# A two-layer sequence model on one Trainium2 core: in later blocks of the state-space scan, time steps and decays laid out by (head, token tile), with rows spread by transfers

## The chip, the cores and the metric

The kernel runs on one core of one Trainium2 chip, as one launch. The metric is device time in microseconds (us). The kernel before took 1160.8 us (median of three runs, 1160.18 to 1161.01). One further execution was profiled: 1159.44 us, of which the profile covers a span of 1157.7 us from the first to the last instruction. Engines are named as in the profile: PE (matmul), PEld (its weight loads), DVE (VectorE), ACT (ScalarE), POOL (GpSimd), SP (SyncE, which here only issues transfers).

## The reference, cut to what matters

The model has two layers, each a sequence mixer and a feed-forward part with residual additions and layer norms between them. The change touches only the mixer of layer 0, a state-space scan with 16 heads of width 64 and a state of 16:

```
zxbcdt = hidden @ W_in                  # gate (1024), xBC (1056), dt (16 heads)
xBC  = silu(causal_conv4(xBC))          # x: 16 heads x 64; B: 16; C: 16
dt   = softplus(dt + dt_bias)
dA   = exp(dt * -exp(A_log))            # one decay per token and head
h    = h * dA[t] + (dt[t] * x[t]) B[t]  # state 64 x 16 per head, over 1024 tokens
y[t] = h . C[t]
y    = (y + D_skip * x) * silu(gate);  y = rmsnorm(y) * norm_w;  out = y @ W_out
```

There are 2 sequences of 1024 tokens, so 2048 tokens. All values are float32.

## The kernel before, in words

The tokens are worked on in four blocks of 512 (b = 0 to 3; blocks 0 and 1 are the first sequence, 2 and 3 the second). A block has four token tiles of 128. The recurrence is computed tile by tile: within a tile the scan becomes a matrix product with a lower-triangular matrix of decay products per head, and a state H (64 x 16 per head) is carried from tile to tile.

For each block these parts exist, written as Python generators so that their steps can be woven into each other:

- `head(b)` turns the input (L211), projects B, C and dt (L332, `pbc`) and copies them to `rows` (L338, called rpad in the trace: 48 partitions, B in 0 to 15, C in 16 to 31, dt in 32 to 47). `mix()` runs the convolution of B and C (L243) and its SiLU into `BC`. Then the time steps are turned to tokens on partitions by four small PE transposes (`pdt`, L355), the bias is added (L359), softplus runs on a [128 x 64] tile in 14 DVE instructions and one of ACT (L187 to L198), and the exponent `a` is formed (L364 to L370). Four more transposes (`pa`, L374) turn `a` back to heads on partitions, ACT takes the exponential (L376, `dA`), four DVE scans form the running products `cum` inside each token tile (L388), `dA` with each tile's first column set to zero is written to DRAM (`decays`, L393), and `cum` is split into a rounded and a rest part in `rc` (L395, L398).
- `project(b)` loads the decays of every head back from DRAM, each spread over 128 partitions (L489, four transfers of 1 MB into `L`). It projects the 1024 channels of x in eight steps `inner(m)` (PE L315 `px`, ACT L413 and L285, the convolution on DVE L243 three times, SiLU L291). Between them stand `crows()` (one PE matmul `pc`, L419, and an ACT copy spread C to 128 partitions as CT), `grams()` (the products of B and C, `pgm` L429, and the transposes of B, `pbt` L430), `spans()` (two PE matmuls `pe`, L444, spread `cum` to 8 heads x 16 states; DVE multiplies by CT to give `cdec`, L448, and copies the tile ends to `over`, L449), and, for four heads at a time, `scans()` (ACT copies L to PSUM, L459; DVE scans it against a stacked identity, L465, giving the decay matrices) and `weigh()` (`bdec` on DVE, L475; four POOL multiplies of L by the gram matrix `gm`, L480).
- `recur(b)` does the four token tiles: `py` takes the state through `cdec` (L585) and the tile's own tokens through L (L593), `pst` gives the new state (L603), DVE updates H (L610, L617) and y (L624), and `by_token` prepares the next tile (PE L562, DVE L564, POOL L568).
- `gates(b)` projects the gate (PE L315 `pg`, ACT L635); `gate(b)` multiplies (DVE L643), squares (ACT L645) and sums (POOL L647); `conclude(b)` applies W_out (PE L658 `po`, L667 `pss`), the norm (L671 to L673), layer norm and the store to `x_mid`.

The order of the work: in block 0 (`opening`) PE, DVE and ACT keep the order in which the program is written. From block 1 on a planner orders every queue at compile time by program order and by its own estimate of when operands are ready, and each engine then runs its queue in that order. The steps are woven by hand: `project(b)` is filled with the steps of `conclude(b - 1)`, and `recur(b)` with two steps of `gates(b)` to one of `head(b + 1)`. So the head of block b + 1 runs in the recurrence of block b. PSUM is one pool of eight banks that all parts share; the tags `tmp` (six buffers) and `rows` (two) are shared as well.

Parameters are loaded at the start by SP, ACT and POOL. POOL then builds the identity matrix (masks.py:197, 199), and PE runs 14 matmuls on it (L165) before it turns the first input.

Of the kernel before, what the change touches and what calls it, by code (L numbers as in the profile page):

```python
# [37 lines left out]
def model_kernel(ctx: ExitStack, tc: tile.TileContext, t: dict, out: bass.AP):  # L38
# [6 lines left out]
    xout = out.rearrange("b (k j p) d -> (b k) p j d", p=P, j=NJ)  # L45
    x_mid = tc.dram_tile([NBLK, P, NJ, D], F32, name="x_mid")
    decays = tc.dram_tile([NBLK, NH, TB], F32, name="decays")

    cp = ctx.enter_context(tc.tile_pool(name="const", bufs=1))
    sp = ctx.enter_context(tc.tile_pool(name="small", bufs=2))  # L50
# [52 lines left out]
    cbr = cp.tile([NBC, 1], F32, tag="cbr", name="cbr")  # L103
    nc.gpsimd.dma_start(cbr, cb_src[DI : DI + NBC].rearrange("(p o) -> p o", o=1))
    skips = row("L0_attn_D_skip", NH, dma=nc.gpsimd)
    nc.sync.dma_start(X[1], xin[1])
    w_out = op.tile([P, NX, D], F32, tag="w_out", name="w_out")
    nc.sync.dma_start(w_out, t["L0_attn_W_out"].rearrange("(m p) o -> p m o", p=P))
# [57 lines left out]

    def exponents():
        endless = cp.tile([P, NH], F32, tag="endless", name="endless")  # L170
        nc.vector.tensor_scalar(endless, alog, EXP_MAX, LOG_FLOOR, ALU.is_gt, ALU.mult)
        rootA = cp.tile([P, NH], F32, tag="rootA", name="rootA")
        nc.vector.tensor_scalar(rootA, alog, EXP_MAX, None, ALU.is_le)
        nc.vector.tensor_tensor(rootA, rootA, alog, ALU.mult)
        nc.scalar.activation(rootA, rootA, AF.Exp, scale=0.5)
        rootN = cp.tile([P, NH], F32, tag="rootN", name="rootN")
        nc.vector.tensor_scalar(rootN, rootA, -1.0, None, ALU.mult)
        return endless, rootA, rootN


    def softplus(o, z, n):

        def tmp(k):
            return sp.tile([P, n], F32, tag=f"sp{k}", name=f"sp{k}", bufs=1)

        e, r, s, s2, p = (tmp(k) for k in range(5))
        nc.vector.scalar_tensor_tensor(e, z, -1.0, z, ALU.mult, ALU.min)  # L187
        nc.scalar.activation(e, e, AF.Exp)
        nc.vector.tensor_scalar(r, e, 2.0, None, ALU.add)
        nc.vector.reciprocal(r, r)  # L190
        nc.vector.tensor_tensor(s, e, r, ALU.mult)
        nc.vector.tensor_tensor(s2, s, s, ALU.mult)
        nc.vector.tensor_scalar(p, s2, 1.0 / 15.0, None, ALU.mult)
        for d in (13, 11, 9, 7, 5, 3):
            nc.vector.scalar_tensor_tensor(p, p, 1.0 / d, s2, ALU.add, ALU.mult)
        nc.vector.scalar_tensor_tensor(p, p, 1.0, s, ALU.add, ALU.mult)
        nc.vector.tensor_scalar(r, z, 0.0, None, ALU.max)
        nc.vector.scalar_tensor_tensor(o, p, 2.0, r, ALU.mult, ALU.add)  # L198
# [122 lines left out]
    def head(b, st):  # L321

        if b >= 3:
            X.append(tokens())
            nc.sync.dma_start(X[b], xin[b])
        xT = st["xT"] = transposed(mp, b, X, bufs=2, by_act=b > 0)[0]

        pm = bank("pbc")
        half = TB // 2
        for k in range(NK):  # L330
            for i in range(2):
                nc.tensor.matmul(  # L332
                    pm[i * 64 : i * 64 + NR, :half], w_in[:, k, 2 * DI : IN_DIM],
                    xT[:, k, i * half : (i + 1) * half], start=(k == 0), stop=(k == NK - 1),
                )
        rows = mp.tile([P, 3 + TB], F32, tag="xpad", name="rpad", bufs=3)
        for i in range(2):
            nc.scalar.copy(  # L338
                rows[:NR, 3 + i * half : 3 + (i + 1) * half], pm[i * 64 : i * 64 + NR, :half]
            )  # L340
        BC = st["BC"] = mp.tile([NBC, TB], F32, tag="BC", name="BC")

        mix = started(rows[:, 3:], NBC, b, NX, cwr, cbr, BC, rows)
        if b < 2:
            yield
        if b:
            mix()
            yield

        z = sp.tile([P, NJ, NH], F32, tag="z", name="z")  # L350
        dt = st["dt"] = sp.tile([P, NJ, NH], F32, tag="dt", name="dt")
        a = sp.tile([P, NJ, NH], F32, tag="a", name="a")
        pdt = bank("pdt")
        for j in range(NJ):
            nc.tensor.transpose(  # L355
                pdt[:, j * NH : (j + 1) * NH], rows[32:NR, 3 + j * P : 3 + (j + 1) * P],
                ident[32:NR, 32:NR],
            )
        nc.vector.tensor_tensor(  # L359
            z, pdt[:, : NJ * NH].rearrange("p (j h) -> p j h", h=NH),  # L360
            dtb.unsqueeze(1).to_broadcast([P, NJ, NH]), ALU.add,
        )
        softplus(dt.rearrange("p j h -> p (j h)"), z.rearrange("p j h -> p (j h)"), NJ * NH)
        nc.vector.tensor_tensor(a, dt, rootA.unsqueeze(1).to_broadcast([P, NJ, NH]), ALU.mult)  # L364
        nc.vector.scalar_tensor_tensor(
            a, a, 1.0e18, rootN.unsqueeze(1).to_broadcast([P, NJ, NH]), ALU.min, ALU.mult
        )
        nc.vector.tensor_tensor(a, a, endless.unsqueeze(1).to_broadcast([P, NJ, NH]), ALU.min)
        for lo in (0, 32):
            nc.vector.tensor_scalar(a2[:, :, lo : lo + NH], a, LOG_FLOOR, None, ALU.max)  # L370
        yield
        pa = bank("pa")
        for j in range(NJ):
            nc.tensor.transpose(pa[:NR, j * P : (j + 1) * P], a2[:, j, :], ident)  # L374
        dA, cum = tmp("dA")[:NR], tmp("cum")[:NR]
        nc.scalar.activation(dA, pa[:NR, :], AF.Exp)  # L376
        if b == 0:

            r = st["r"] = mp.tile([NR, TB], F32R, tag="rows", name="rows", bufs=2)
            nc.scalar.activation(r, pa[:NR, :], AF.Exp)  # L380
            yield
            nc.vector.tensor_tensor(r[32:NR], dA[32:NR], r[32:NR].bitcast(F32), ALU.subtract)
            nc.vector.memset(r.bitcast(F32).rearrange("r (j t) -> r j t", t=P)[:, :, 0:1], 0.0)
            mix()
            yield
        for j in range(NJ):
            w = slice(j * P, (j + 1) * P)
            nc.vector.tensor_tensor_scan(  # L388
                cum[:, w], dA[:, w], zeros[:NR].to_broadcast([NR, P]), 1.0, ALU.mult, ALU.add
            )  # L390
        if b:
            nc.vector.memset(dA.rearrange("r (j t) -> r j t", t=P)[:, :, 0:1], 0.0)
            nc.sync.dma_start(decays[b], dA[:NH])  # L393
        rc = st["rc"] = mp.tile([NR, TB], F32R, tag="rows", name="rows", bufs=2)
        nc.scalar.copy(rc, cum)  # L395
        if b == 0:
            yield
        nc.vector.tensor_tensor(rc[32:NR], cum[32:NR], rc[32:NR].bitcast(F32), ALU.subtract)  # L398
        yield

    def parts(b, st):
# [21 lines left out]
        def grams():  # L423

            pgm = bank("pgm")
            pbt = bank("pbt")
            for j in range(NJ):
                s = slice(j * P, (j + 1) * P)
                nc.tensor.matmul(pgm[:, s], BC[:NS, s], st["CT"][:NS, s], start=True, stop=True)  # L429
                nc.tensor.transpose(pbt[:, j * NS : (j + 1) * NS], BC[:NS, s], ident[:NS, :NS])  # L430
            st["gm"] = mp.tile([P, TB], F32, tag="gm", name="gm")
            nc.scalar.copy(st["gm"], pgm)
            st["bt"] = sp.tile([P, NJ, NS], F32, tag="bt", name="bt", bufs=1)
            nc.vector.tensor_copy(
                st["bt"], pbt[:, : NJ * NS].rearrange("p (j n) -> p j n", n=NS)
            )

        def spans():

            cdec = st["cdec"] = mp.tile([P, 2, TB], F32, tag="cdec", name="cdec")  # L440
            over = st["over"] = sp.tile([P, 2, NJ], F32, tag="over", name="over")
            for q in range(2):
                pe = bank("pe")
                nc.tensor.matmul(  # L444
                    pe, pickn[:, 8 * q : 8 * q + 8, :].rearrange("r h n -> r (h n)"), st["rc"],
                    start=True, stop=True,
                )
                nc.vector.tensor_tensor(cdec[:, q, :], pe, st["CT"], ALU.mult)  # L448
                nc.vector.tensor_copy(  # L449
                    over[:, q, :].unsqueeze(2),  # L450
                    pe.rearrange("p (j t) -> p j t", t=P)[:, :, P - 1 : P],
                )

        def scans(h0):

# [28 lines left out]
    def project(b, st):  # L484
# [6 lines left out]
                decays[b, h0 : h0 + 4].rearrange("h t -> (h t)").partition_broadcast(P),  # L491
            )
        inner(0)()
        crows()
        yield
        inner(1)()
        yield
        grams()
        inner(2)()
        yield  # L500
        spans()
        for m in range(3, NX):
            inner(m)()
            if m < 7:
                scans(4 * m - 12)
                weigh(4 * m - 12)
            yield
# [175 lines left out]
    with tc.manual_schedule(  # L683
        engines={mybir.EngineType.PE, mybir.EngineType.DVE, mybir.EngineType.Activation}
    ):
        next(own)
        endless, rootA, rootN = exponents()
        next(own)
        cwx, cbx, normw, dskip = columns_of_layer()
        opening(st, own, g, ahead)  # L690
# [506 lines left out]
```

## Time and profile before

| | us |
|---|---|
| median of the runs | 1160.8 |
| the profiled execution | 1159.44 |
| its span | 1157.7 |
| block 0's opening, about | 0 to 72 |
| recurrence of block 0 | 72 to 103 |
| projection of block 1 | 103 to 167 |
| recurrence of block 1 | 167 to 214 |
| projection, recurrence of block 2 | 214 to 277, 277 to 324 |
| projection, recurrence of block 3 | 324 to 386, 386 to 430 |
| end of the first mixer and all that follows | 430 to 1158 |

The stretches are read from the order of time on PE. In the profile's timeline a line gives the start, the duration, the engine and line of the program, the operation, what it writes and reads, its shape and how many such instructions are merged; in brackets stands idle time of the engine just before and what ended it. A float32 matmul of 512 columns shows as two records, so eight records of L315 are one step of four matmuls. Matmuls are pipelined, so the printed durations of neighbours overlap, and the distance between starts is what one takes of PE's time.

### The profile page before, as it was taken

The page shows a single profiled execution, that of the slowest core. Times are in us where ns is not written, and L with a number is a line of the kernel's source. Part 1 is how long each engine was busy: PE and PEld are TensorE (multiplying, and loading weights), DVE is VectorE, ACT ScalarE, POOL GpSimd, SP SyncE. Part 2 cuts the span into 40 slices and gives each one's busy share as a digit, 9 for nine tenths or more (in the row PEclk, how much of TensorE's full clock was granted, in tenths as well). Part 3 has the DMA queues.
Part 4 walks back from the last instruction along what each step waited for, and adds up shares of the span by engine and source line. Part 5 has one row for each costly group of instructions (what it writes and reads, how often), then busy time and mean ns, then how long its engine had stood idle before and what let it go on. Part 6 is the DMA issues. An engine that isn't in the chain of part 4 may idle for free.

```text
span 1157.7 us, 12317 instructions
## 1 busy us (share of the span) xinstructions
PE 1129.0 (98%) x4659; PEld 686.0 (59%) x4659; DVE 680.7 (59%) x1248; ACT 461.8 (40%) x705; POOL 351.4 (30%) x339
## 2 busy tenths in 40 slices
PE   8999999999999999999999999999999999999995
PEld 5455445445644555654444444447888888888884
DVE  5897795697569756873626328073228765225224
ACT  3334533562354233456645382543223223223222
POOL 1546371445146440367122212237401001001002
PEclk9999999999999999999999999999999999999998
DMA  9003001300030028203000000003501000001001
GB/s 331 2 1 147 1 1 74 147 0 37 1 147 1 37 91 257 99 1 119 0 1 0 1 1 0 1 0 118 182 1 37 1 1 37 1 1 37 1 1 39
DMA packets 30451, 56.46 MB, mean 49 GB/s; under 512 B 11480, under 2 KB 11512, under 8 KB 27824
## 3 DMA queue, kind: packets, MB, share of 16 engines
q1 hardware_dynamic: 29424, 55.45, 13.6%
q8 instruction: 38, 0.62, 0.2%
q14 instruction: 29, 0.24, 0.1%
q10 hardware_dynamic: 864, 0.14, 0.1%
q0 software_dynamic: 96, 0.01, 0.0%
HBM read 47.11 MB, written 8.49 MB: 48 GB/s over the span
## 4 chain that ended last, share of the span: by engine, by line
PE 78%; DVE 15%; ACT 4%; issue 2%; POOL 1%; DVEq 0%; ACTq 0%; POOLq 0%
PE pgu L1041 21%; PE p L890 17%; PE po L1064 10%; PE pg L315 8%; PE px L315 5%; DVE L L465 4%; PE po L967 4%; DVE acc L243 4%; PE po L658 3%; PE py L593 2%; PE po L839 2%; PE pt L211 1%; PE pxt L562 1%; DVE xc L643 1%; DVE st L230 1%
## 5 line engine op out<-in xcount | busy, mean ns | idle before, releaser
L1050 DVE SCALAR_TENSOR_TENSOR h<-pgu,L_ffn_up_scale,sg 128x512 f32<-128x512 f32 x64 | 47.9, 749 | 149.7 <-PE pgu L1041 145.5
L480 POOL TENSOR_TENSOR L<-L,gm 128x512 f32<-128x512 f32 x64 | 93.2, 1485 | 79.6 <-DVE bdec L475 49.6
L315 PE MATMUL px<-xT,w_in 128*128 128x512 f32 x256 | 117.1, 605 | 0.2 <-DVE over L449 0.2
L658 PE MATMUL po<-w_out,xc 128*128 128x512 f32 x256 | 112.6, 593 | 2.0 <-DVE L L465 2.0
L315 PE MATMUL pg<-xT,w_in 128*128 128x512 f32 x256 | 113.5, 594 | 0.0
L890 PE MATMUL p<-xT,w 128*128 128x512 f32 x256 | 112.1, 593 | 1.4 <-ACT xT L220 1.4
L890 PE MATMUL p<-cv,w 128*128 128x512 f32 x256 | 111.0, 592 | 0.0
L1064 PE MATMUL po<-wd,hh 128*128 128x512 f32 x256 | 101.4, 396 | 0.0
L1041 PE MATMUL pgu<-wF__4499,wg 128*128 128x512 f32 x256 | 101.3, 396 | 0.0
L1064 PE MATMUL po<-wd,hl 128*128 128x512 f32 x256 | 101.3, 396 | 0.0
L1041 PE MATMUL pgu<-wF__4499,wu 128*128 128x512 f32 x256 | 101.0, 394 | 0.0
L1041 PE MATMUL pgu<-lo__4500,wg 128*128 128x512 f32 x256 | 100.8, 394 | 0.0
L1041 PE MATMUL pgu<-lo__4500,wu 128*128 128x512 f32 x256 | 100.7, 393 | 0.0
L1048 ACT ACTIVATE sg<-pgu,L_ffn_gate_scale 128x512 f32<-128x512 f32 x64 | 44.0, 687 | 133.3 <-PE pgu L1041 133.2
L1056 ACT CAST hh<-h 128x512 fp32r<-128x512 f32 x64 | 39.8, 621 | 118.5 <-DVE h L1050 118.3
L658 PEld LDWEIGHTS po<-w_out,xc 128*128 128x128 f32 x256 | 48.3, 190 | 63.4 <-issue 55.9
L890 PEld LDWEIGHTS p<-cv,w 128*128 128x128 f32 x256 | 48.4, 190 | 59.8 <-issue 58.8
L315 PEld LDWEIGHTS px<-xT,w_in 128*128 128x128 f32 x256 | 48.0, 193 | 60.5 <-issue 56.8
L890 PEld LDWEIGHTS p<-xT,w 128*128 128x128 f32 x256 | 48.5, 190 | 58.7 <-issue 55.2
L243 DVE SCALAR_TENSOR_TENSOR acc<-xpad,cols,acc 128x512 f32<-128x512 f32 x72 | 68.8, 963 | 18.8 <-ACT acc L285 18.0
L315 PEld LDWEIGHTS pg<-xT,w_in 128*128 128x128 f32 x256 | 47.4, 190 | 54.3 <-issue 53.6
L1138 POOL TENSOR_TENSOR x<-x,r 128x512 f32<-128x512 f32 x12 | 15.2, 1298 | 206.3 <-DVE r L1137 206.3
(239 smaller groups left out, 1944.3 us busy)
## 6 DMA issues: line engine op xcount, KB each, us to landing
L<-decays SPq DMA_DIRECT2D x12, 1024.0 KB, 8.6
x_mid<-x SPq DMA_DIRECT2D x4, 1024.0 KB, 3.8
x<-x_mid SPq DMA_DIRECT2D x4, 1024.0 KB, 4.9
st<-in_L_ffn_gate_w_dram SPq DMA_DIRECT2D x8, 512.0 KB, 4.7
st<-in_L_ffn_up_w_dram SPq DMA_DIRECT2D x8, 512.0 KB, 4.4
st<-in_L_ffn_down_w_dram SPq DMA_DIRECT2D x8, 512.0 KB, 4.0
x<-_attn_hidden_states_dram SPq DMA_DIRECT2D x3, 1024.0 KB, 9.7
out_dram<-x SPq DMA_DIRECT2D x3, 1024.0 KB, 4.3
```

The costliest lines, as they stand in the source:

```text
L243: nc.vector.scalar_tensor_tensor(acc, xpad[:, k : k + TB], w[:, k : k + 1], acc, ALU.mult, ALU.add)
L315: nc.tensor.matmul(pm[:n, :], w_in[:, k, lo : lo + n], xT[:, k, :], start=(k == 0), stop=(k == NK - 1),)
L465: nc.vector.tensor_tensor_scan(L[:, h, :], pl, id4.rearrange("p j t -> p (j t)"), 0.0, ALU.mult, ALU.add)
L480: nc.gpsimd.tensor_tensor(L[:, h, :], L[:, h, :], st["gm"], ALU.mult)
L658: nc.tensor.matmul(po, xc[:, m, j * P : (j + 1) * P], w_out[:, m, :], start=(m == 0), stop=(m == NX - 1),)
L890: nc.tensor.matmul(pm, w1[:, i, k, m * P : (m + 1) * P], rhs[:, k, :], start=(k == 0), stop=(k == NK - 1),)
L967: nc.tensor.matmul(po, y[:, k, j * P : (j + 1) * P], w1[:, 4, k, :], start=(k == 0), stop=(k == NK - 1),)
L1041: nc.tensor.matmul(pm, w[g][:, k, cols], x[:, k, :], start=(k == 0 and x is pieces[0]), stop=(k == NK - 1 and x is pieces[-1]),)
L1048: nc.scalar.activation(sg, pgu[0], AF.Silu, scale=gs[:, m : m + 1])
L1050: nc.vector.scalar_tensor_tensor(h, pgu[1], us[:, m : m + 1], sg, ALU.mult, ALU.mult)
L1056: nc.scalar.copy(hh, h)
L1064: nc.tensor.matmul(po[j], x[:, j * P : (j + 1) * P], wd[m // GK][:, m % GK, :], start=(m == 0 and x is h[0]), stop=(m == NF - 1 and x is h ...
```

## The change

For blocks 1 to 3:

- The dt rows are copied by a transfer inside SBUF from [16 heads, 512 tokens] to `turn`, [64 partitions = (head, token tile), 128 tokens]. Bias, softplus, exponent and exponential run there (`by_rows`), with parameters as columns on those 64 partitions (`by_hj`, loaded at the start by two POOL transfers). One DVE scan gives all running products. They go to DRAM (`since`), and the decays as before.
- The rows of B are copied to the other 64 partitions of `turn`, and one PE transpose (`ptk`) gives both the time steps and B by token (`tk`), in place of the `pdt`, `pa` and `pbt` transposes.
- C goes to DRAM (`crow`) and is read back spread over 128 partitions as CT, in the tag `rows`; the matmul `pc` and its copy go.
- `spans()` reads the running products from `since`, spread to 8 heads x 16 states, straight into `cdec` (two transfers of 256 KB); the `pe` matmuls go, and so do `rc` and its split. The multiply by CT is done on POOL, in place, and `spans()` is called in step m = 6 of the projection, ahead of the last `scans` and `weigh`, and not before step 3.

Block 0 keeps its way; some of its tiles get other buffers.

```diff
+    HJ = NH * NJ
+    by_hj = cp.tile([HJ, 5], F32, tag="by_hj", name="by_hj")
+    for i, name in enumerate(("L0_attn_dt_bias", "L0_attn_A_log")):
+        nc.gpsimd.dma_start(
+            by_hj[:, i : i + 1], t[name].unsqueeze(1).to_broadcast([NH, NJ]).unsqueeze(2)
+        )
...
+        if b:
+            turn = mp.tile([P, P], F32, tag="a2", name="turn")
+            nc.sync.dma_start(
+                turn[:HJ], rows[32:NR, 3:].rearrange("h (j t) -> h j t", t=P)
+            )
         if b < 2:
             yield
         if b:
             mix()
+            nc.sync.dma_start(turn[HJ:], BC[:NS].rearrange("n (j t) -> n j t", t=P))
+            nc.sync.dma_start(crow[b], BC[NS:])
+            st["CT"] = mp.tile([P, TB], F32, tag="rows", name="CT", bufs=2)
+            nc.sync.dma_start(st["CT"], crow[b].unsqueeze(0).to_broadcast([8, NS, TB]))
             yield
+            yield from by_rows(b, turn, tk)
+            return
...
+    def by_rows(b, turn, tk):
+        z, work = turn[:HJ], [tmp(f"work{i}")[:HJ] for i in range(2)]
+        e, r, s, s2, p, a, dA, cum = (
+            w[:, i : i + P] for w in work for i in range(0, TB, P)
+        )
+        if b == 1:
+            exponents(*(by_hj[:, i : i + 1] for i in range(1, 5)))
+        bias, _, end, rA, rN = (by_hj[:, i : i + 1] for i in range(5))
+        nc.vector.tensor_scalar(z, z, bias, None, ALU.add)
+        softplus(z, z, P, (e, r, s, s2, p))
+        nc.vector.tensor_scalar(a, z, rA, 1.0e18, ALU.mult, ALU.min)
+        nc.vector.tensor_scalar(a, a, rN, end, ALU.mult, ALU.min)
+        nc.vector.tensor_scalar(a, a, LOG_FLOOR, None, ALU.max)
+        nc.scalar.activation(dA, a, AF.Exp)
+        nc.vector.tensor_tensor_scan(
+            cum, dA, zeros[:HJ].to_broadcast([HJ, P]), 1.0, ALU.mult, ALU.add
+        )
+        nc.sync.dma_start(since[b].rearrange("h (j t) -> (h j) t", t=P), cum)
+        nc.vector.memset(dA[:, 0:1], 0.0)
+        nc.sync.dma_start(decays[b].rearrange("h (j t) -> (h j) t", t=P), dA)
+        yield
+        pt = bank("ptk")
+        nc.tensor.transpose(pt[:, :P], turn, ident)
+        nc.vector.tensor_copy(tk, pt[:, :P].rearrange("p (v n j) -> p v j n", v=2, j=NJ))
+        yield
...
             for q in range(2):
-                pe = bank("pe")
-                nc.tensor.matmul(
-                    pe, pickn[:, 8 * q : 8 * q + 8, :].rearrange("r h n -> r (h n)"), st["rc"],
-                    start=True, stop=True,
-                )
-                nc.vector.tensor_tensor(cdec[:, q, :], pe, st["CT"], ALU.mult)
...
+                h = slice(8 * q, 8 * q + 8)
+                if b:
+                    nc.sync.dma_start(
+                        cdec[:, q, :], since[b, h].unsqueeze(1).to_broadcast([8, NS, TB])
+                    )
+                    pe = cdec[:, q, :]
...
+                ends = pe.rearrange("p (j t) -> p j t", t=P)[:, :, P - 1 : P]
+                if b:
+                    nc.vector.tensor_copy(over[:, q, :].unsqueeze(2), ends)
+                    nc.gpsimd.tensor_tensor(pe, pe, st["CT"], ALU.mult)
...
         inner(0)()
-        crows()
         yield
...
-        spans()
         for m in range(3, NX):
             inner(m)()
+            if m == 6:
+                spans()
             if m < 7:
                 scans(4 * m - 12)
                 weigh(4 * m - 12)
```

## The prediction

> **What bounds the kernel now.** I read the page's busy table first, then the waits of PE, then the chain that ended last, then PE's, DVE's and POOL's order of time through the later scan blocks, and last the first ten microseconds.
>
> ```profile
> PE 1129.0 (98%) x4659; PEld 686.0 (59%) x4659; DVE 680.7 (59%) x1248; ACT 461.8 (40%) x705; POOL 351.4 (30%) x339
> ```
>
> PE is busy for 1129.0 of 1157.7 us. The list of PE's waits adds up to about 16 us, of which 3.8 lie before its first instruction. So whatever leaves PE's queue shortens the kernel, as long as no other engine is equally late at that place. The busy times by stretch (columns: window, its length, then PE, PEld, DVE, ACT, POOL busy with instruction counts, granted clock, DMA share, GB/s) say where one is:
>
> ```profile
> 130.00:160.00 30.00, 29.33 (x69) 12.85 (x68) 29.96 (x37) 13.77 (x24) 20.46 (x16) 1.00 0.00 0
> 170.00:214.00 44.00, 44.00 (x320) 25.60 (x313) 26.75 (x67) 16.47 (x25) 8.43 (x10) 1.00 0.20 75
> ```
>
> The second row is the recurrence of block 1 (`recur`): PE 44.00 of 44.00, DVE 26.75. PE alone sets the pace. The first is the second half of its projection (`project`): PE 29.33 and DVE 29.96 of 30.00, both full. There an edit must relieve both engines. Blocks 2 and 3 repeat these rows within 0.1 us (240 to 270, 350 to 380, 280 to 324).
>
> **What leaves PE.** In block 2 the order of time on PE reads (start, duration, line; DVE's first span multiply is added):
>
> ```profile
> 214.09 3.60 PE L315 MATMUL px<-xT,w_in 128*128 128x512 f32 x8
> 217.61 1.12 PE L419 MATMUL pc<-BC,pickc 32*128 32x512 f32 x2
> 218.66 3.70 PE L315 MATMUL px<-xT,w_in 128*128 128x512 f32 x8
> ...
> 234.13 0.95 PE L667 MATMUL pss<-ones,sums 128*128 128x1 f32 x8
> 235.00 0.73 PE L444 MATMUL pe<-rows,pickn 48*128 48x512 f32 x2
> 235.54 0.69 DVE L448 TENSOR_TENSOR cdec<-pe,CT 128x512 f32<-128x512 f32 x1 [2.10 <-PE pe L444]
> 235.67 7.13 PE L315 MATMUL px<-xT,w_in 128*128 128x512 f32 x16
> ```
>
> Printed durations overlap their neighbours (the matmuls are pipelined), so I cost each by the distance between starts. The spread of C (`pc`): 218.66 - 217.61 = 1.05 us. The spread of running products (`pe`, two matmuls): 235.67 - 235.00 = 0.67. The four little transposes of B (`pbt`) stand between the `pgm` matmuls; the chain gives each 0.02, its own record 0.17, so 0.1 to 0.7 together; I take 0.2, near the chain, since the next `pgm` starts 0.03 us after each. In the recurrence the four `pdt` add 0.23 (192.87 until `py` runs alone at 193.10), the four `pa` 0.53 (204.03 to 204.56). The one new transpose `ptk` costs 0.12 in a stream (16 `pt` take 1.91) and at most the 0.33 of an isolated `pxt`; I take 0.15.
>
> - Projection: 1.05 + 0.2 + 0.67 = 1.92 a block, 5.8 for three.
> - Recurrence of the block before, where the next head is prepared: 0.23 + 0.53 - 0.15 = 0.61, times three 1.8.
> - One wait: in block 1 PE stood 1.56 us at L429 for CT, because ACT's copy of CT came behind the squares of the gate. CT now comes by transfer during the recurrence before. Its two hops are priced by the write of `decays` (2.9 us) and a 256 KB load with little beside it (3.5 us), and over 20 us lie between. That is 1.6, once. What is late next there is PE's own stream.
>
> **What that does to DVE in the full stretch.** The two `cdec` multiplies and `over` copies (0.69 + 0.15 + 0.68 + 0.13 = 1.65 us) stood before the first scan. The multiplies go to POOL, the copies (0.28) come back later. DVE also starts earlier by what left PE ahead of `pss`, 1.25. Its end moves by 1.25 + 1.65 - 0.28 = 2.6 against PE's 1.9: a reserve of 0.7 a block. [...]
>
> ```profile
> 135.27 6.88 POOL L480 TENSOR_TENSOR L<-L,gm 128x512 f32<-128x512 f32 x4 [15.33 <-DVE bdec L475]
> 136.85 2.40 DVE L243 SCALAR_TENSOR_TENSOR acc<-xpad,cols,acc 128x512 f32<-128x512 f32 x2
> 140.31 0.72 DVE L243 SCALAR_TENSOR_TENSOR acc<-xpad,cols,acc 128x512 f32<-128x512 f32 x1
> 159.30 6.29 POOL L480 TENSOR_TENSOR L<-L,gm 128x512 f32<-128x512 f32 x4 [2.15 <-DVE bdec L475]
> 161.80 4.33 DVE L243 SCALAR_TENSOR_TENSOR acc<-xpad,cols,acc 128x512 f32<-128x512 f32 x3 [0.31 <-ACT acc L285]
> ```
>
> A convolution step takes 0.72 us while POOL pauses between multiplies, 1.2 to 1.45 beside them. The four scans at 144.51 took 4.55 beside a POOL burst, the usual 1.14 each: they read PSUM and are spared. The two new POOL multiplies last 1.49 each (mean of L480), so they cost DVE between 0 (in POOL's idle 119.9 to 135.3, where DVE has gaps of 2 us) and 2 x 1.49 = 3.0 a block. I take 1.2, since `spans` is called late (m = 6), yet the planner does move work forward: the input load of L325 for block 3 went out at 179.18, a whole block ahead of its place. Less the reserve of 0.7 that is 0.5 a block, 1.5 in all.
>
> [...]
>
> **DVE, ACT and transfers in the recurrence.** The softplus works on 64x128 instead of 128x64. Some 19 instructions grow from 0.22 to about 0.29 (slope of two-input operations: 0.68 for 512, 0.42 for 256 elements), the reciprocal from 0.55 to about 1.0: +1.8. Four scans (1.36) become one (0.34), and the difference of the rounded rows (0.68) goes: -1.7. This nets to nothing and lies in DVE's 17 us of idle in that stretch. Block 1 adds `exponents` on 64 partitions, four DVE instructions of 0.18 and one of ACT (0.20), beside PE. ACT loses two copies and gains nothing.
>
> SP issues seven more transfers a block (two for `turn`, `crow`, CT, `since`, two for `cdec`), 0.32 to 0.45 of its own time each. They pass the x_mid store and stand ahead of the L loads. `decays` itself leaves one step earlier, and so can L; L lay ready some 15 us before its first scan (landing at most 10.8 after its issue at 98.25 to 100, scans from 128.49), so neither the one nor the other moves the end. The turned time steps land some 3 us after the row copy (182.78), by the 2.9 us of `decays`; DVE reached `z` at 193.33 before. Behind `z` on DVE wait the state updates at 186.76 to 188.4, which PE needs at 192.9: 4.4 us of cover. I cost this at nothing.
>
> **The start.** Two parameter transfers are added to POOL's queue ahead of the identity:
>
> ```profile
> 1.27 0.73 POOL L102 DMA_DIRECT2D cwr<-in_L_attn_conv_w_dram  x1 [0.82 <-POOLq L1182]
> 2.00 0.51 POOL L104 DMA_DIRECT2D cbr<-in_L_attn_conv_b_dram  x1
> 2.50 0.58 POOL L86 DMA_DIRECT2D L_attn_D_skip<-in_L_attn_D_skip_dram  x1
> ...
> 3.40 0.32 POOL masks.py:199 TENSOR_SCALAR_AFFINE_SELECT ident<-ident 128x128 f32<-128x128 f32 x1
> 3.78 4.77 PE L165 MATMUL early<-ident 128*128 128x128 f32 x28 [3.78 <-POOL ident masks.py:199]
> 8.38 1.91 PE L211 MATMUL pt<-ident,x 128*128 128x128 f32 x16
> ```
>
> PE's first matmuls follow the identity without a gap, and the input's transposes follow those without a gap. Two more issues of 0.51 to 0.73 move all of it by 1.0 to 1.5; if the input (second half issued at 1.26, landing near 7) is not the limit, nothing hides that. A later wait for w_in could swallow it (0 as the other end). I take 1.1.
>
> **The sum.** -5.8 - 1.8 - 1.6 + 1.5 + 1.1 = -6.6 us. The profiled execution took 1159.44 us (span 1157.7), so its like becomes 1152.8; it is 1.4 below the median of the runs, 1160.8, which becomes 1154.2. I predict **1154 us**.
>
> **Rivals.**
> 1. *DVE is freed altogether.* The products fall into POOL's idle time, and the reserve removes PE's waits in the full stretch (0.67 for a scan's bank and about 0.7 for the last convolution, 4.1 over three blocks). For it: the early X load. Then 1154.2 - 1.5 - 4.1 = 1148.6, and 1147.5 with the start hidden.
> 2. *The turned rows come late.* If DVE's planned order puts `z` before the state updates, and the transfer takes the 9.7 us of the 1 MB input loads instead of 2.9, it lands at 192.7, the updates end near 194.5, and PE waits 1.6 a block, 4.8 in all, with 0.4 more at the start: 1159.4, no measurable change. Against it: only one block has such a load beside it, and DMA's share was 0.22 at 183 to 186.
> 3. *Slower: POOL's queue at the end of the scan stretch.* If the two products stand directly ahead of the last four L480, they run beside that stretch's convolutions, DVE loses the 2.3 beyond its reserve, the last burst starts that much later still, and POOL's gap of 2.15 before it doesn't hold 2 x 1.71 (a multiply beside convolutions). The burst ended at 165.6, and PE reads heads 12 to 15 from about 168.8. The projection then ends about 2.5 later than now instead of 1.9 earlier: 3 x 2.5 - 1.8 - 1.6 + 1.1 = +5.2, 1166. It decides from 1.5 a block on. For it: `spans` at m = 6, ahead of the last `weigh`. Against: cdec and CT are loaded early, and POOL idles 15 us before.
> 4. *PE's removal does nothing there* because DVE alone sets the end: then the projection follows DVE, which this change relieves too, and rivals 1 and 3 bound it.
>
> **Numbers.** Forecast 0.50; rival 1 0.17; rival 2, or an unforeseen order with the same effect, 0.15; rival 3 0.16; something else, slower, 0.02. The bound for no measurable change is 0.2%, 2.3 us. Faster 0.67, same 0.15, slower 0.18. The range takes in rival 1 down to 1148 and rival 3 nearly up to its price, 1165; forecast and rival 1 by themselves span 1147.5 to 1158.
>
> **What would show it.** PE's busy time falls by about 7 us, with L419, L444, L430, L355 and L374 gone for blocks 1 to 3; no wait for CT; POOL's two span products early in the projection (right) or directly before the last L480 (rival 3); the identity about 1 us later; no DVE wait on `turn`. The forecast is wrong if PE shows new waits on transfers, on POOL or on convolutions of 3 us or more a block, or if the planner's new order opens gaps elsewhere.

## The result, and the profile after

The changed kernel takes 1149.76 us (median of four runs, 1148.89 to 1150.88) against 1160.9 for the kernel before in the same comparison: ratio 0.9909, 95% interval 0.9897 to 0.992, or 11.1 us less. The profiled execution took 1149.05 us (span 1147.2), 10.4 less than the profiled one before. The prediction said 1154 in a range of 1148 to 1165: the direction was right, the gain 1.7 times the sum's 6.6.

The busy line of the page, and the same two stretches as before the change by engine (window, length, PE, PEld, DVE, ACT, POOL busy, granted clock, DMA share, GB/s):

```profile
PE 1118.7 (98%) x4614; PEld 684.2 (60%) x4614; DVE 678.9 (59%) x1228; ACT 459.0 (40%) x700; POOL 361.9 (32%) x347
```

```profile
130.00:160.00 30.00, 27.94 (x65) 11.99 (x64) 29.90 (x38) 15.33 (x27) 20.78 (x16) 1.00 0.00 0
170.00:214.00 44.00, 44.00 (x314) 25.41 (x315) 30.18 (x66) 18.23 (x28) 11.72 (x12) 1.00 0.33 119
```

PE's busy time fell by 10.3 us, nearly all of the gain; its idle time in the span is 28.5 us instead of 28.7, so the waits that went and those that came are about equal. But block 1's full stretch (first row) holds less PE work than before, 27.94 instead of 29.33, with DVE as full as ever: there PE now waits. The order of time on PE in block 2:

```profile
213.65 7.03 PE L323 MATMUL px<-xT,w_in 128*128 128x512 f32 x16
220.61 1.15 PE L474 MATMUL pgm<-CT,BC 16*128 16x128 f32 x8
...
232.10 0.95 PE L724 MATMUL pss<-ones,sums 128*128 128x1 f32 x8
232.91 7.11 PE L323 MATMUL px<-xT,w_in 128*128 128x512 f32 x16
```

`pc`, `pbt` and `pe` are gone. From the first `px` to `pgm` lie 6.96 us instead of 8.20, from `pss` to the next `px` 0.81 instead of 1.54. POOL's new products stand early, in its idle time, as rival 1 had it and not rival 3:

```profile
215.60 1.26 POOL L506 TENSOR_TENSOR cdec<-cdec,CT 128x512 f32<-128x512 f32 x1
223.06 1.27 POOL L506 TENSOR_TENSOR cdec<-cdec,CT 128x512 f32<-128x512 f32 x1 [0.86 <-DVE over L505]
```

At the start the identity is 1.04 us later, and DVE stands at the head of its queue for `by_hj`, ahead of what PE's first projection needs:

```profile
3.57 0.55 POOL L112 DMA_DIRECT2D by_hj<-in_L_attn_A_log_dram  x1
4.82 6.19 PE L174 MATMUL early<-ident 128*128 128x128 f32 x28 [4.82 <-POOL ident masks.py:199]
10.00 0.14 DVE L179 TENSOR_SCALAR by_hj<-by_hj 64x1 f32<-64x1 f32 x1 [8.92 <-DMA by_hj<-in_L_attn_A_log_dram]
10.84 1.91 PE L219 MATMUL pt<-ident,x 128*128 128x128 f32 x16
```

The first `px` starts at 16.12 instead of 13.66. In this profile PE is these 2.46 us late already at the transposes, 10.84 instead of 8.38: 1.04 from the identity, and 1.42 because the 28 first matmuls take 6.19 instead of 4.77. The second part does not come with the new loads: in the kernel with C alone by transfer (below), whose POOL queue is as before, they take 6.03. DVE's stand would have cost about as much by itself. In three kernels below that have it too but shorter first matmuls (4.82, 5.05, 5.37), PE waits 1.05, 1.16 and 0.60 for `xT` behind them, and the first `px` starts at 15.87 to 16.22 all the same.

And in block 0, where nothing was to change, the planner put block 1's turned steps among the last convolutions, because their rows now land early:

```profile
66.32 0.27 DVE L427 TENSOR_SCALAR turn<-turn,by_hj 64x128 f32<-64x128 f32 x1
70.92 0.94 DVE L198 RECIPROCAL work<-work 64x128 f32<-64x128 f32 x1
74.92 0.33 PE L619 MATMUL pxt<-ident,xc 128*128 128x128 f32 x1 [2.44 <-ACT xc L316]
75.18 3.41 PE L650 MATMUL py<-L,dtx 128*64 128x128 f32 x32
```

PE waits 2.44 us for the last SiLU (0.68 before), and the `py` behind it takes 3.41 instead of 2.26: the granted clock is 0.50 from 76 to 78 us.

The same PE instruction's start, before minus after, tells where the 10 us came from: -2.5 at the first `px`, -3.8 at block 0's `pst`, -2.4 at block 1's first `px`, +0.4 at block 2's, +4.9 at block 3's, +8.7 at the end of the first mixer and through the second, +10.1 at the last matmul. So the later blocks gain well over the sum, the first 75 us lose more than it, and 1.3 us appear in the last 360 us, where the program is the same.

### The profile page after: what moved, and what is told of

It is laid out like the page before. It is cut to its first block, busy times and chain, and to the rows that moved or that the text cites. A ratio compares the mean times of both kernels' runs of the same rounds, so it can differ in the third digit from the quotient of the medians.

```text
span 1147.2 us, 12259 instructions
## 1 busy us (share of the span) xinstructions
PE 1118.7 (98%) x4614; PEld 684.2 (60%) x4614; DVE 678.9 (59%) x1228; ACT 459.0 (40%) x700; POOL 361.9 (32%) x347
## 4 chain that ended last, share of the span: by engine, by line
PE 84%; DVE 10%; ACT 4%; issue 1%; POOL 0%; DVEq 0%; ACTq 0%; POOLq 0%
PE pgu L1098 21%; PE p L947 17%; PE po L1121 10%; PE pg L323 9%; PE px L323 7%; PE po L715 6%; PE po L1024 4%; PE py L650 3%; DVE acc L251 2%; PE po L896 2%; DVE L L522 2%; PE pxt L619 1%; PE pt L219 1%; DVE xc L700 1%; PE py L642 1%
## 5 line engine op out<-in xcount | busy, mean ns | idle before, releaser
L323 PE MATMUL px<-xT,w_in 128*128 128x512 f32 x256 | 114.6, 597 | 0.2 <-DVE over L509 0.2
```

Source lines behind the costliest of these rows:

```text
L323: nc.tensor.matmul(pm[:n, :], w_in[:, k, lo : lo + n], xT[:, k, :], start=(k == 0), stop=(k == NK - 1),)
```

## The experiments

Times are medians; positions are starts of one PE instruction in the profiles, compared with the changed kernel's.

**The start alone, on the kernel before.** Two loads as large as `by_hj`'s, into scratch:

```diff
+    for i, name in enumerate(("L0_attn_dt_bias", "L0_attn_A_log")):
+        nc.gpsimd.dma_start(L[: NH * NJ, 2 + i, 0:1], ...)
     ident = cp.tile([P, P], F32, tag="ident", name="ident")
```

> The kernel before, with two small extra loads on POOL's queue ahead of the identity, into scratch that is written again before it is read; nothing else. Theory (a late identity costs more than its delay, since TensorE's first matmuls then run slower as well): first px matmul 1.5 to 2.5 us later than in the kernel before (13.66 us there), identity done near 4.8 us, median +1.0 to +2.5 us. Rival A (only the delay counts, as the prediction had it): first px +1.0 us, median +0.5 to +1.0. Rival B (the opening waits for its own loads, the identity is hidden): within 0.5 us.

Measured 1161.33, ratio to before 1.0007 (0.9998 to 1.0016); identity at 4.82, first `px` at 14.81, 1.15 late; last matmul 1.3 late. The medians alone do not tell this from nothing; in the profiles Rival A fits: the delay counts once, and no more. The identity is as late here as in the changed kernel, and the first matmuls take 4.88, not 6.19. So the other 1.3 us of the changed kernel's late `px` are not the identity's.

**Loads behind the identity, and DVE's first steps on them behind the opening's.**

```diff
-    for i, name in enumerate(...): nc.gpsimd.dma_start(by_hj[...], ...)
     nc.gpsimd.memset(eps, LN_EPS)
+    for i, name in enumerate(...): nc.gpsimd.dma_start(by_hj[...], ...)
-        nc.vector.tensor_scalar(endless, alog, ...)
+        tc.keep_in_program_order(nc.vector.tensor_scalar(endless, alog, ...))
```

> The changed kernel, with the two loads of by_hj behind the identity on POOL's queue and its first DVE steps behind the opening's. Theory: identity done near 3.8 us again, the 28 early transposes 4.6 us instead of 6.0, first px near 13.7 instead of 16.1 us, and the gain carried to the end, 0.8 to 2.5 us below the changed kernel (about 1147.3 to 1149). Rival A (the delay alone): -0.5 to -1.0. Rival B (DVE sets the first block's end, so an earlier start of TensorE is lost there): within 0.5 us.

Measured 1149.61, no gain; a miss. The identity comes at 4.27 only, the first `px` at 14.67; the 1.45 us last until 35 us and are gone at 72, where this profile is 0.66 behind. Between lies a stretch of half clock (0.75 and 0.50 at 38 to 42 us), which the changed kernel's profile does not have and the one before has. Its length is 3.4 us, its price 1.7.

**Block 1's turned steps held behind the opening.**

```diff
-        if b == 1: exponents(...)
-        nc.vector.tensor_scalar(z, z, bias, None, ALU.add)
+        shifted = nc.vector.tensor_scalar(z, z, bias, None, ALU.add)
+        if b == 1:
+            tc.keep_in_program_order(shifted)
+            exponents(...)
```

> The changed kernel, with block 1's steps on (head, token tile) rows held on DVE behind the first block's last convolutions and dtx. Theory (DVE's turned steps, 2 to 3 us of them, sit among those convolutions and TensorE waits for the last SiLU, 2.4 us at pxt in block 0): that wait falls back to about 0.7, pst of block 0 is done 2 to 3.5 us earlier, median 2 to 3.5 us below the changed kernel, about 1146.3 to 1147.8. Rival (the scan stretch of block 1 is set by DVE's total and not by where the steps stand): the wait goes, but comes back at block 1's po or pxt, median within 0.7 us.

Measured 1146.81 (ratio to before 0.9887, 0.9872 to 0.9902), 2.9 below the changed kernel.

```profile
73.25 0.33 PE L620 MATMUL pxt<-ident,xc 128*128 128x128 f32 x1 [0.70 <-ACT xc L316]
73.50 2.26 PE L651 MATMUL py<-L,dtx 128*64 128x128 f32 x32
```

The wait is 0.70 again, `py` takes 2.26 at full clock, `pst` is done 2.83 earlier, and all of it stays to the end (2.93). Shown: the early turned steps cost 2.9 us, of which 1.75 are the wait itself and 1.2 the slowed `py`. Steps that are ready early are not free where they are put. That the slow `py` follows from the wait is read from both going together.

**Both edits.**

> The changed kernel with both edits: loads of by_hj behind the identity, and block 1's turned steps behind the first block's convolutions. Theory: the two gains add, as they lie at different places of TensorE's queue: 3 to 5 us below the changed kernel, about 1145 to 1147. Rival (DVE is the bound of the first two blocks, so only one of them counts): 0.5 to 2.5 us below, no more than the better of the two alone.

Measured 1147.79: no better than the second alone. In this profile the start's 1.57 us are lost again between 35 and 72 us, to the same stretch of half clock. Up to here the rival (an earlier start is refunded) stood as well as the theory.

**Products on DVE instead of POOL.**

```diff
-                    nc.gpsimd.tensor_tensor(pe, pe, st["CT"], ALU.mult)
+                    nc.vector.tensor_tensor(pe, pe, st["CT"], ALU.mult)
```

> The changed kernel with its four span products a block (64 x 128 running products times C) on DVE instead of POOL, at the same place in the order of tracing. Theory (TensorE's queue sets the end of a block, and DVE has some slack behind its convolutions once pa, pdt, pbt and the running products are off TensorE): 4 x about 1 us more on DVE a block, of which half comes to light: +0 to +4 us against the changed kernel, and TensorE's waits for the gate's L grow. Rival (the gain is DVE's relief in the scan stretch, rival 1 of the prediction): all of it comes to light, +8 to +12 us, most of the change's gain gone.

Measured 1148.73, in the profile 0.47 ahead of the changed kernel, all of it in block 1, where the first wait for L falls from 1.05 to 0.47; blocks 2 and 3 are the same to 0.01. On DVE a product takes 0.69 instead of POOL's 1.26 to 1.76. The medians' intervals overlap (0.9888 to 0.9922 here). Both theories had it slower. It refutes the rival: the gain does not come from sparing DVE these products.

**C through TensorE and ACT again.** `crows()` as before for all blocks, the transfers `crow` and CT left out.

> The changed kernel with C spread to its 128 rows by TensorE and ACT again for blocks 1 to 3 (the kernel before's way), all else as changed. Theory: one projection matmul of 0.26 x 4 us a block comes back on TensorE, +1.05 us a block, and no stand at pgm to remove: +2.5 to +4 us against the changed kernel. Rival (the transfers of C and the turned rows hinder each other or the loads, so taking them out pays for the matmuls): -1 to +1 us. Rival (what the change took from TensorE counts double, since it stands in for a DVE wait): +5 us and more.

Measured 1153.96, 4.2 above the changed kernel (3.2 in the profile); by the median between the bounds of the theory and the second rival. Blocks 2 and 3 lose 1.25 each, as `pc` and its neighbours' wider spacing cost. Block 1 loses more, and the order of time on PE and the clock say why:

```profile
113.21 1.68 PE L471 MATMUL pgm<-CT,BC 16*128 16x128 f32 x8 [1.69 <-ACT CT L463]
114.82 6.50 PE L323 MATMUL px<-xT,w_in 128*128 128x512 f32 x8
```

```profile
114.00:116.00 2.00, 2.00 (x7) 1.26 (x6) 1.96 (x2) 0.00 (x0) 1.67 (x2) 0.50 0.00 0
```

Behind the wait of 1.69 the clock is half for 6.8 us, and eight records of `px` take 6.50 instead of 3.70. (In this order the turned steps cost block 0 less: the wait there is 1.58, with no such stretch.)

**Products and copies held where they are traced (m = 6), rival 3's place.**

```diff
+                    tc.keep_in_program_order(
                         nc.vector.tensor_copy(over[:, q, :].unsqueeze(2), ends)
+                    )
+                    tc.keep_in_program_order(
                         nc.gpsimd.tensor_tensor(pe, pe, st["CT"], ALU.mult)
+                    )
```

> The changed kernel with the span products on POOL and their copies on DVE held at the place where they are traced, among the last bursts of L times the decays. Rival 3 of the prediction had this as the slower case: two pairs of products of 2 x 1.3 to 1.8 us each ahead of the last bursts, +2.5 to +5 us a block, +7 to +15 us. Theory now (POOL has slack behind its bursts, since TensorE reaches po later than DVE and POOL are done): 0 to +4 us against the changed kernel. A gain is excluded by neither where the stall of 1.4 us on DVE behind the early products goes: down to -2 us.

Measured 1151.74, 2.0 above the changed kernel (2.9 in the profile).

```profile
161.56 2.93 POOL L509 TENSOR_TENSOR cdec<-cdec,CT 128x512 f32<-128x512 f32 x2
167.43 0.33 PE L623 MATMUL pxt<-ident,xc 128*128 128x128 f32 x1 [1.86 <-ACT xc L299]
168.34 3.45 PE L654 MATMUL py<-L,dtx 128*64 128x128 f32 x32
```

The products do stand amid the last burst, and the wait for the last SiLU grows from 0.65 to 1.86. But rival 3 had priced this at 2.5 a block behind the old end; here blocks 2 and 3 lose 0.46 and 0.31 against the changed kernel, and block 1 loses 1.7 net, with a stretch of half clock of about that price behind its wait. Even in rival 3's order the change would have been a gain.

**Time steps as before the change, C and products spread by transfer.** No `by_hj`, no `turn`, four scans, `pdt`, `pa` and `pbt` on PE.

> The changed kernel with time steps and decays on (head) rows again, four scans and the transposes through TensorE as in the kernel before; C and the running products still come by transfer, the products are still POOL's. Theory: lost are pbt's and the recurrence's terms (0.35 + 0.6 us a block, 2 to 3 us in all), won back the late start (1 to 2.5 us) and the steps among the first block's convolutions (2 to 3.5 us): between -3 and +1 us against the changed kernel. Rival (the turned form relieves DVE enough to set the end): +4 us and more.

Measured 1154.16, 4.4 above the changed kernel: as much as the rival said. With the products by transfer, the turned form is worth more than PE's transposes. From block 2 of this kernel:

```profile
238.62 7.13 PE L675 MATMUL po<-w_out,xc 128*128 128x512 f32 x16 [0.47 <-DVE L L482]
253.63 7.13 PE L675 MATMUL po<-w_out,xc 128*128 128x512 f32 x16 [1.01 <-DVE L L482]
...
214.33 1.14 DVE L465 COPY over<-cdec 128x4 f32<-128x4 f32 x1 [2.77 <-DMA cdec<-since]
217.25 1.73 DVE L660 TENSOR_TENSOR xc<-xc,g 128x512 f32<-128x512 f32 x1 [1.18 <-ACT g L652]
220.89 3.57 DVE L245 SCALAR_TENSOR_TENSOR acc<-xpad,cols,acc 128x512 f32<-128x512 f32 x3 [1.91 <-ACT acc L287]
```

DVE ends the previous block's gate at 219.0 and begins block 2's convolutions 9.45 us behind its first `px` (211.44). In the kernel before that is 7.22, in the changed kernel 5.68, in the last kernel below 6.49. So this mixture is worse there than the kernel before, and the reason stands in its rows: amid the gate DVE waits 0.76 and 2.77 for the spread running products. Their rows leave for DRAM at 205.50 here, behind the four scans, and at 198.21 in the changed kernel. DVE then trails PE through the scan stretch, and PE waits for it; in the changed kernel's blocks 2 and 3 these waits for L are gone. Part of the 4.4 is thus the price of products that come late, and not what the turned form is worth against the kernel before.

**The tile `by_hj` alone, on the kernel before.** Loaded as in the change, never read, with one buffer of `z` so that it fits.

> The kernel before with the tile by_hj of the changed kernel and its two loads ahead of the identity, never read, and one buffer of z instead of two; nothing else. After the 782 us mark the two kernels run the same instructions, and yet all seven changed-kernel variants with this tile run that tail 1.33 to 1.38 us shorter in the profile than the three kernels without it (the one before, that with the loads into scratch, that with the old time steps). Theory (where the tail's tiles lie in memory makes its matmuls 0.4% faster, and this tile shifts them): tail 1.2 to 1.5 us shorter than before, so that with a start price of 0.7 the median is -0.3 to -1.0 us against before. Rival (the tail's rate comes from something else that the turned steps bring): tail as before, median +0.5 to +1.2 us, as with the loads into scratch.

Measured 1160.16 (ratio to before 0.9996, 0.9987 to 1.0005). The part behind 782 us runs 1.27 shorter than in the kernel before, though the program there is the same: from 784.07 to the last matmul's end 361.98 us, in the kernel before from 781.98 363.25. Its matmuls of 512 columns follow one another in 231.1 to 233.7 ns on average by kind instead of 231.8 to 234.1. Without the tile the same part takes 363.27 with the two loads into scratch, 363.30 with old time steps (which has the one buffer of `z` too) and 363.24 with C alone. Shown: that part's gain comes with the tile, and not with the new steps. That it acts by where later tiles lie, as the theory has it, was not shown; which tile's place would matter was not tried. By the medians the kernel is as before; in the profile the late start outweighs this gain by 0.82 us at the last matmul.

**C alone by transfer, on the kernel before.**

```diff
             mix()
+            nc.sync.dma_start(crow[b], BC[NS:])
+            st["CT"] = tmp("CT")
+            nc.sync.dma_start(st["CT"], crow[b].unsqueeze(0).to_broadcast([8, NS, TB]))
...
-        crows()
```

> The kernel before with C alone spread by transfer in blocks 1 to 3; time steps, decays and running products as before. Theory (the parts add: putting C back on TensorE cost the changed kernel 4.2 us, old time steps 4.4 us, so C is worth about 4 and the products' transfer the rest of 5.8, 1.5 to 2): 3.2 to 4.5 us below before, about 1155.5 to 1156.8. Rival (pc's matmuls only, 1.05 x 3 and no wait, since DVE then sets the scan stretch): 1.5 to 2.5 us below. Rival (the parts help each other, none is worth much alone): under 1.5 us.

Measured 1154.19, 6.2 below before, a larger gain than the theory's 3.2 to 4.5. In the profiles 0.35 of the 4.8 us gained by the end of the mixer lie ahead of block 0's `pst`; the rest, 4.5, is 2.0 in block 1 and 1.24 in each of blocks 2 and 3, as the theory has it. The medians differ by over 1 us more than the profiles: the profiled execution of the kernel before, 1159.44, is 1.0 below its median here.

**The two that helped.** Turned steps held (2.9) and products on DVE.

> The changed kernel with block 1's turned steps held behind the first block's convolutions (2.9 us shorter alone) and the span products on DVE instead of POOL (0.5 us shorter in its profile, 1.0 in its median). Theory (the second acts on block 1's wait for L at po, 1.10 us in the kernel with the first alone, and leaves 0.5 of it): 3.2 to 4.2 us below the changed kernel, about 1145.5 to 1146.5, the fastest of all. Rival (with the steps held behind, DVE reaches the last scans no earlier and its own products only add to them): 1.5 to 2.8 us below, no better than the first alone.

Measured 1146.17, 3.6 below the changed kernel, inside the theory's range, but not clear of the first edit alone (1146.81; the intervals overlap). In block 1 the first wait for L is 0.47, as expected.

**And the start, without POOL.** In addition the `by_hj` loads go to ACT's queue, behind ACT's own loads, and DVE's first steps on them are held.

```diff
-        nc.gpsimd.dma_start(
+        nc.scalar.dma_start(
             by_hj[:, i : i + 1], t[name]...
```

> The changed kernel with the two edits of the fastest so far (turned steps of block 1 held behind the first block's convolutions, span products on DVE), and the two loads of by_hj issued by ACT behind its own parameter loads instead of by POOL ahead of the identity, with DVE's first steps on by_hj behind the opening's. Theory (what the start costs is the identity's 1.04 us and DVE's stand for by_hj, and the rest of what the executions show there is the clock's half-speed stretch near 40 us, which comes or stays away by its own phase): identity done near 3.8, first px between 13.7 and 15.0 us instead of 16, and 0.5 to 1.5 us below the kernel without this edit (1146.17), when the half-speed stretch is the same in both; a half-speed stretch more or less is 1.7 us either way. Rival (the start is refunded by that stretch, an earlier start always brings it): no gain, 1146 to 1147.5, and a half-speed stretch between 36 and 43 us in the profile.

Measured 1144.86 (1144.43 to 1145.18; ratio to before 0.9866, 0.985 to 0.9883), the fastest of all, 4.9 below the changed kernel.

```profile
3.78 4.83 PE L174 MATMUL early<-ident 128*128 128x128 f32 x28 [3.78 <-POOL ident masks.py:199]
13.73 2.84 PE L327 MATMUL px<-xT,w_in 128*128 128x512 f32 x6
```

This profile and the one of the kernel without this edit both have the stretch of half clock near 40 us, so they compare like with like: 2.25 earlier at `px`, 2.21 at the end of the mixer. The start's price is real in the profiles; the medians differ by 1.3, and their intervals overlap. Of the 2.25, 1.04 are the identity and 1.21 lie between the identity and the first projection, where the first matmuls (4.83 instead of 5.37) and DVE's stand (PE waits 0.60 for `xT` without the edit) come together. The start's price was hidden in the changed kernel's profile because that one had no such stretch near 40 us; on what this depends was not shown.

## Why the prediction was right, and where its sum was wrong

By part, gains positive, in the profiles' us. "Measured" is the experiment that isolates the part:

| part | predicted | measured | from |
|---|---|---|---|
| C by transfer (`pc`, CT wait) | 3.15 + 1.6 | 4.5 | C alone, from block 0's `pst` on |
| running products by transfer (`pe`, contention) | 2.0 - 1.5 | 1.6 | old time steps, less C alone, from block 0's `pst` on; the medians (1154.16, 1154.19) show no difference |
| turned time steps (`pbt`, `pdt`, `pa`) | 0.6 + 1.8 | 6.7 | last kernel against old time steps from block 0's `pst` on (7.2), less 0.5 for products on DVE; holds what the late products cost the old time steps |
| late start | -1.1 | -0.8 in that profile, -2.2 like with like | last two kernels |
| turned steps among the opening's | 0 | -2.9 | steps held |
| tail | 0 | 1.3 | the tile alone |
| sum | 6.6 | 10.4 | the two profiled executions: 10.4 |

The rows are measured in one order, C first, and what one part makes possible for another falls to the later one: the products and the turned steps together (8.3) are firmer than either row. That the sum meets 10.4 is in part luck: the first three rows make 12.8, while the changed kernel gains 12.5 from block 0's `pst` to block 3's, and 0.4 of the 10.4 lie behind the last matmul.

- **Projection, 1.92 a block: right in kind, a little small.** `pc` 1.24 (1.05, and about 0.2 in the spacing of the `px` on both sides), `pbt` 0.35 where I took 0.2 of 0.1 to 0.7, `pe` 0.73: 2.3.
- **Recurrence, 0.61 a block: right.** 0.57 and 0.56 in blocks 1 and 2's recurrences.
- **The CT wait: right.** PE's 1.56 are gone; the transfers land in time.
- **Contention of POOL and DVE, +0.5 a block: the failed term, together with "a reserve of 0.7".** It was an estimate between nothing and the two products' whole length, and no run shows it: products on DVE leave blocks 2 and 3 unchanged to 0.01 us, so on either engine they cost nothing at the end there. The reading behind the term was off too: "1.2 to 1.45" are means of merged rows. Between 134 and 166 us of the kernel before, single convolution steps take 0.72 to 0.98 or 1.64 to 1.76, and POOL's multiplies 1.26 to 1.28 or 1.66 to 1.82.
- **"This nets to nothing and lies in DVE's 17 us of idle": with the reserve, the step that cost most of the miss.** For DVE's time in the recurrence it held. But DVE gains more than the sum allowed on its way to the last convolutions. Counted from the block's first `px`, its first scan stands 5.10 and 4.75 us earlier than before in blocks 2 and 3, and its last convolution ends 4.67 and 4.34 earlier (2.30 in block 1), where the sum had 2.6. A part is DVE's entry: the previous block's gate is finished earlier, and the convolutions of block 2 begin 5.68 behind `px` instead of 7.22, those of block 3 4.93 instead of 5.53. The waits that I let stand go. Block 2 before:

```profile
221.31 3.58 DVE L243 SCALAR_TENSOR_TENSOR acc<-xpad,cols,acc 128x512 f32<-128x512 f32 x3 [1.91 <-ACT acc L285]
257.20 7.13 PE L658 MATMUL po<-w_out,xc 128*128 128x512 f32 x16 [0.67 <-DVE L L465]
276.09 0.33 PE L562 MATMUL pxt<-ident,xc 128*128 128x128 f32 x1 [0.69 <-ACT xc L291]
276.74 2.13 PE L593 MATMUL py<-L,dtx 128*64 128x128 f32 x32 [0.31 <-POOL xc L568]
```

and after, where 0.62 remain that no engine explains:

```profile
219.33 3.57 DVE L251 SCALAR_TENSOR_TENSOR acc<-xpad,cols,acc 128x512 f32<-128x512 f32 x3 [1.91 <-ACT acc L293]
272.41 2.13 PE L650 MATMUL py<-L,dtx 128*64 128x128 f32 x32 [0.62 <-issue]
```

  That stop before cost 0.16 more than its listed length: `po` at 257.20 stood for 0.67 and came 0.83 late (7.70 behind the start of the `px` ahead of it, after the change 6.87). From block 2's first `px` to block 3's it is 105.14 us instead of 109.59, 4.45 less: 2.32 in the projection's matmuls, 0.83 at this `po`, 0.61 from `pxt` to `pst`, 0.56 in the recurrence, 0.13 elsewhere; the sum had 1.92 + 0.61 - 0.5. This is rival 1's mechanism, reached by the time steps and the planner's order more than by the products' new engine. With C alone the convolutions of block 2 begin 7.21 behind `px`, as before, so the earlier entry comes with the time steps and products. Whether the shorter work, rows that leave earlier or the new order of the gate did it, these runs don't separate.
- **The start, +1.1: right for the identity (1.04), too small for the start.** I priced POOL's queue and not DVE's, where the planner put first what waits for the load: with that order `px` does not start before 15.87 in any profile. In the changed kernel's own profile the slow first matmuls alone reach as far.
- **"It lands early enough" (rival 2): it landed too early.** The harm was the opposite of the one I weighed: ready steps were moved forward, into block 0's critical convolutions. I had the sign of this in hand, a load that went out a whole block ahead, and used it for POOL only.
- **Rival 3** did not occur, and its price was wrong too: its order costs 0.3 to 0.5 a block over the early one, and 1.7 where the clock falls, where it had 2.5 + 1.9.
- **DVE alone sets the end (rival 4)** holds in block 1 only: 1.5 us ahead of before at 125, level at 165. The late opening does not explain it: in the last kernel block 1 begins 3.84 us earlier, and the waits for L stand there at 0.48 and 1.01, as with the products on DVE alone.

The result lies inside the range because the two errors of the later blocks (too little gain) and of the first (too little loss) partly cancelled. That is luck in part: with block 1's early steps held, and nothing else, the kernel took 1146.81, below the range. And 1149.76 lies nearer to rival 1's 1148.6, to which I gave 0.17, than to the forecast's 1154.2.

## What to carry to other kernels

A planner that orders by readiness turns every operand that comes earlier into a new order: ask of each newly early instruction which critical stretch it can be pulled into, on every engine, and pin it if that stretch is critical. Where two engines are both full, price an edit on the engine that trails at the moment it enters the stretch; time freed long before it can be worth more than what is freed in it. Compare stage by stage, on one instruction's start, and check that both profiles have the same clock stretches before a difference is given to an edit.

## What the runs showed of the hardware

Some short stops of PE cost more than themselves. Behind waits of 1.69 us (`pgm` at 113.21 with C through TensorE again), 1.86 (`pxt` at 167.43 with the products held) and 2.44 (`pxt` at 74.92 in the changed kernel, at 75.58 with the loads behind the identity) the granted clock fell to 0.50, the first time for 6.8 us and otherwise for 3.4, a price of 3.4 and 1.7. Behind waits of 1.56 (`pgm` at 113.11 before the change), 1.58 (`pxt` at 73.81 with C through TensorE again) and 1.66 (`po` at 768.54 before the change and at 759.82 after it) it stayed at 1.00. The same 3.4 us at half clock stood between 37 and 50 us in eight of the fourteen profiles and not in six. The 28 first matmuls took 4.77 us before the change and 6.19 after it: they followed one another in 0.21 us up to the first record of a full clock in the trace, which comes 2.9 and 5.9 us behind the first of them, and in 0.11 after it.

The clock's records of these two profiles give the places. Before the change the first record of a full clock begins at 6.70 us, and the half clock lasts from 37.42 to 40.83; after it they stand at 10.71 and from 75.56 to 78.97. Both stretches are 3.41 us long and begin 30.72 and 64.85 us behind that first record, 9 and 19 times their length. The run of small matmuls in the opening goes from 34.03 to 37.55 before the change and from 36.48 to 39.99 after it, each with one listed stop of 0.17 at its end; half clock begins at the end of the first and not of the second. What decides between the two these runs do not show.

A tile of five numbers a partition, never read (with one buffer of another small tile less), shortened an unchanged stretch behind 782 us by 1.27 of 363 us, 0.35%; why is not shown.
